# A gated recurrence on one Trainium2 core: the update gate's product with the state in seven half products, and one subtraction on GpSimd

## The chip, the core and the metric

The kernel runs on one core of one Trainium2 chip. Its engines are called as the profile calls them: PE (TensorE, the matrix engine), PEld (PE's weight loads), DVE (VectorE), ACT (ScalarE), POOL (GpSimd) and SP (the engine that issues most DMAs). The metric is the device time of one launch in microseconds (us), as the median of the runs.

## The reference, cut to what matters

The reference is one decoder layer in float32: causal self attention, then a slot attention with a gated recurrence (three rounds over the same 2048 rows of 256 features), then a mixture of experts. Only the recurrence matters here. Per round and per batch element:

```python
q_proj = rmsnorm(slots) @ Wq.T
scores = einsum('bkd,bmd->bkm', q_proj, k_proj) * SCALE
attn   = softmax(scores, axis=-2)                    # over the slots
attn   = attn / (sum(attn, axis=-1) + EPS)
updates = einsum('bkm,bmd->bkd', attn, v_proj)
# gru_cell(updates, slots):
gx = updates @ wih.T + bih          # split into xr, xz, xn
gh = slots @ whh.T + bhh            # split into hr, hz, hn
r = sigmoid(xr + hr)
z = sigmoid(xz + hz)
n = tanh(xn + r * hn)
slots = (1.0 - z) * n + z * slots
```

`slots` is 8 x 256 x 256 and the context `P` is 8 x 120 x 256, so an attention row has 120 entries.

## The kernel before, in words

**Stages.** Self attention fills the first 385 us of the profile, the recurrence the stretch from there to about 660 us, and the mixture of experts the rest.

**The recurrence in phases.** The rows lie feature-major in four blocks `XT[i]`, each 128 partitions x 2 chunks of features x 512 columns (two batch elements of 256). A phase `p` is one round for one block, so there are 12 phases, in the order round 0 block 0, 1, 2, 3, round 1 block 0, and so on. Phase `p` updates block `p % 4`, and a block is read again four phases later; its norm and scores are worked out two phases ahead (`norms(p + 2)`, `softmax(p + 2)`), its attention shares one phase ahead (`shares(p + 1)`).

The input side is folded: `G` (L773, filled by `given(b)`, L837) holds context x value weights x input weights, so that the product of the attention rows `AT_[p]` (120 x 512) with `G` gives the input part of a gate at once. In `gate(p, g, hidden, given)` (L903) a gate's sum of hidden and given part is built up in PSUM: per output chunk two matmuls of `whh_sb` with `XT[i]` over 512 columns, and two of `G` with `AT_[p]` over 256 columns each. In the profile each float32 matmul is two records.

**Seven products.** For the candidate's hidden part (g = 2) the 2 x 2 blocks of the weight (128 x 128 each) and of the state (128 x 256 each) are multiplied with seven block products instead of eight, in phases 0 to 8 (`SEVEN` = 9, `hidden_seven`, L964). The sums of weight blocks (`hidden_weights`, four POOL instructions into the finished `wih_sb`) are made once, the sums of state blocks (`hidden_states(p)`, four POOL instructions `t1` to `t4`) once a phase, in one of two sets `STATE_SUMS[p % 2]`. Four products go to a PSUM tile `x`, three to a second one `y`; ACT copies the first (L975), and four DVE instructions add the others into `out`, which is an SBUF tile. In phases 9 to 11 the plain `gate` is used.

**PSUM.** The gates and the seven products take tiles of two banks from the pool "big", which has two slots that are handed out in turn. A phase before phase 9 asks for five: the reset gate `r` (L992), `x` and `y` of the candidate, the candidate's given part `p_x` (L1006), and the update gate `p_z` (L1012). Smaller products (`pd`, `pr`, `pz`) use the pool "bk" of four banks.

**Order.** PE and ACT run in program order through the whole kernel (the manual schedule of L270). DVE and POOL do so only in the self attention (L275); in the recurrence the framework's planner orders their instructions when it builds the program, by its own estimate of when each becomes ready, and the engine then runs them in that order. In the profile POOL therefore works ahead: the squares for `norms(p + 3)` and the sums `hidden_states(p + 2)` are run in phase `p`.

**Within phase p**, in program order: `r` gate and its sigmoid (L994); `hidden_states(p + 1)` and `hidden_seven(p)`; the table of exponentials is loaded on ACT (L998); `shares(p + 1)`; L1002 turns `n` into (hn + bhh) * r on DVE; `norms(p + 2)` and `softmax(p + 2)`; `p_x`, added into `n` on DVE (L1007); the table of sigmoid and tanh (L1009); tanh (L1011); `p_z` and its sigmoid (L1014); then three DVE instructions, `r = sT - n`, `r = r * z` and `sT = r + n`, the last of which writes the block.

Of the kernel before, what the change touches and what calls it, by code (L numbers as in the profile page):

```python
# [14 lines left out]
ALU = mybir.AluOpType  # L15
AX = mybir.AxisListType

B, S, D = 8, 256, 256
# [4 lines left out]
P = 128  # L23
DC = D // P
# [3 lines left out]
BPB = BLK // S  # L28
# [37 lines left out]
def decoder_kernel(  # L66
# [23 lines left out]
    nc = tc.nc  # L90
# [6 lines left out]
    def big(name):  # L97
        return pools["big"].tile([P, 2, 512], F32, tag="big", name=name)

    def bank(name):  # L100
        return pools["bk"].tile([P, 512], F32, tag="bk", name=name)
# [38 lines left out]
    for c0 in (0, 256):  # L140
        nc.gpsimd.affine_select(
            out=mask[:, c0 : c0 + P],
# [33 lines left out]
    xwq_sb = const.tile([P, DC, D], F32, name="xwq_sb")  # L176
# [94 lines left out]
    with (  # L271
# [153 lines left out]
        def features(i, m, k):  # L425

            return XT[i][:, k, :].rearrange("p (t m q) -> p t m q", m=2, q=P)[:, :, m, :]
# [11 lines left out]
        def product(i, t, m):  # L439
            if V[i] is None:  # L440
                V[i] = a2.tile([P, NSUB, H * HD], F32, tag="v", name=f"v_{i}")
            pv = bank(f"pv_{i}_{t}_{m}")
            sums = [feature_sums[:, j, :] for j in range(4)]
            a11, a12, a22 = (features(i, *mk)[:, t, :] for mk in ((0, 0), (0, 1), (1, 1)))
            a, b = {
                1: (a11, B11),
                2: (a12, B21),
                3: (sums[3], B22),
                4: (a22, T4),
                5: (sums[0], T1),  # L450
                6: (sums[1], T2),
                7: (sums[2], T3),
            }[m]
            nc.tensor.matmul(pv, a, b, start=True, stop=True)
            c11, c12, c21, c22 = (V[i][:, 2 * t + n, c] for n in range(2) for c in half_cols)
            if m == 1:
                nc.scalar.copy(c11, pv)
            for o, old in {
                2: [(c11, c11)],
                3: [(c12, c12)],  # L460
                4: [(c21, c21)],
                5: [(c12, c22), (c22, c21)],
                6: [(c22, c11)],
                7: [(c21, c22)],
            }.get(m, []):
                nc.vector.tensor_tensor(o, pv, old, ALU.add)
# [176 lines left out]
        for k in range(last + 1):  # L643
            i, j = divmod(k, 2 * NPAIR)
# [50 lines left out]
    for table in (xd, yd):  # L695
# [21 lines left out]
        out=upper,  # L717
# [34 lines left out]
    for h in range(2):  # L752
        n = (NSINGLE + 1 - h) // 2
# [12 lines left out]
    def tt(o, a, b, op):  # L766
        nc.vector.tensor_tensor(o, a, b, op)  # L767
# [5 lines left out]
    G = b1.tile([MC, B, 3 * D], F32, name="G")  # L773
# [74 lines left out]
    RR, AT_ = {}, {}  # L848
# [54 lines left out]
    def gate(p, g, hidden, given):  # L903
        it, i = phases[p]
        pg = big(f"gate_{p}_{g}")
        for oc in range(DC):
            o = ts(DC * g + oc, P)
            if hidden:
                for dc in range(DC):
                    nc.tensor.matmul(  # L910
                        pg[:, oc, :],
                        whh_sb[:, dc, o],
                        XT[i][:, dc, :],
                        start=dc == 0,
                        stop=not given and dc == DC - 1,
                    )
            if given:
                for bi in range(BPB):
                    nc.tensor.matmul(  # L919
                        pg[:, oc, ts(bi, S)],  # L920
                        G[:, BPB * i + bi, o],
                        AT_[p][:, bi, :],
                        start=not hidden,
                        stop=not hidden or bi == BPB - 1,
                    )
        return pg
# [6 lines left out]
    SEVEN = len(phases) - NBLK + 1  # L933
    whh5 = whh_sb.rearrange("p k (g o q) -> p k g o q", o=DC, q=P)
    done = wih_sb.rearrange("p k n -> p (k n)")
    w_sums = done[:, 0 : 4 * P].rearrange("p (j q) -> p j q", q=P)
    STATE_SUMS = (
        [done[:, 4 * P + k * S :][:, 0:S] for k in range(4)],
        [w[:, k, :] for w in (xwk_sb, xwv_sb) for k in range(2)],
# [2 lines left out]
    def pool(o, a, b, op=ALU.subtract):  # L942
        nc.gpsimd.tensor_tensor(o, a, b, op)

    def hidden_weights():
        a11, a12, a21, a22 = (whh5[:, k, 2, o, :] for o in range(DC) for k in range(DC))
        s1, s2, s3, s4 = (w_sums[:, j] for j in range(4))
        pool(s1, a21, a22, ALU.add)
        pool(s2, s1, a11)
        pool(s3, a11, a21)  # L950
        pool(s4, a12, s2)

    def hidden_states(p):
        if p >= SEVEN:
            return
        it, i = phases[p]
        b11, b12, b21, b22 = (XT[i][:, k, ts(n, S)] for k in range(DC) for n in range(BPB))
        t1, t2, t3, t4 = STATE_SUMS[p % 2]
        pool(t1, b12, b11)
        pool(t2, b22, t1)  # L960
        pool(t3, b22, b12)
        pool(t4, b21, t2)

    def hidden_seven(p, out):  # L964
        it, i = phases[p]
        a11, a12, a21, a22 = (whh5[:, k, 2, o, :] for o in range(DC) for k in range(DC))
        s1, s2, s3, s4 = (w_sums[:, j] for j in range(4))
        b11, b12, b21, b22 = (XT[i][:, k, ts(n, S)] for k in range(DC) for n in range(BPB))
        t1, t2, t3, t4 = STATE_SUMS[p % 2]
        c = out.rearrange("p o (n s) -> p (o n) s", n=BPB)  # L970
        x, y = (big(f"seven_{p}_{j}").rearrange("p a (b q) -> p (a b) q", q=S) for j in range(2))
        for j, ab in enumerate(((a11, b11), (s3, t3), (a12, b21), (s2, t2))):
            nc.tensor.matmul(x[:, j], *ab, start=True, stop=True)

        nc.scalar.copy(c[:, 1], x[:, 0])  # L975
        tt(c[:, 0:2], x[:, 2:4], c[:, 1:2].to_broadcast([P, 2, S]), ALU.add)
        tt(c[:, 3], x[:, 1], c[:, 1], ALU.add)
        for j, ab in enumerate(((s4, b22), (a22, t4), (s1, t1))):
            nc.tensor.matmul(y[:, j], *ab, start=True, stop=True)
        tt(c[:, 1:3], y[:, 0:2], c[:, 1:4:2], ALU.add)  # L980
        tt(c[:, 1:4:2], y[:, 2:3].to_broadcast([P, 2, S]), c[:, 1:4:2], ALU.add)

    def phase(p, between):

        it, i = phases[p]
        sT = XT[i]

        def tmp(tag):
            return b2p.tile([P, DC, BLK], F32, tag=tag, name=f"{tag}_{p}")

        r, z, n = tmp("r"), tmp("z"), tmp("n")
        p_r = gate(p, 0, True, True)  # L992
        for oc in range(DC):
            nc.scalar.activation(r[:, oc, :], p_r[:, oc, :], AF.Sigmoid, bias=brz[:, oc : oc + 1])  # L994
        if p < SEVEN:
            hidden_states(p + 1)
            hidden_seven(p, n)
        nc.scalar.preload_act_table_set(LNEXP)  # L998
        between[0]()
        p_h = n if p < SEVEN else gate(p, 2, True, False)  # L1000
        for oc in range(DC):
            nc.vector.scalar_tensor_tensor(  # L1002
                n[:, oc, :], p_h[:, oc, :], bhh[:, 4 + oc : 5 + oc], r[:, oc, :], ALU.add, ALU.mult
            )
        between[1]()
        p_x = gate(p, 2, False, True)  # L1006
        tt(n, p_x, n, ALU.add)  # L1007
        between[2]()
        nc.scalar.preload_act_table_set(SIGTANH)  # L1009
        for oc in range(DC):  # L1010
            nc.scalar.activation(n[:, oc, :], n[:, oc, :], AF.Tanh, bias=bih[:, 4 + oc : 5 + oc])  # L1011
        p_z = gate(p, 1, True, True)  # L1012
        for oc in range(DC):
            nc.scalar.activation(z[:, oc, :], p_z[:, oc, :], AF.Sigmoid, bias=brz[:, 2 + oc : 3 + oc])  # L1014

        tt(r, sT, n, ALU.subtract)
        tt(r, r, z, ALU.mult)
        tt(sT, r, n, ALU.add)
        between[3]()
# [234 lines left out]
    for b in range(B):  # L1254
        given(b)
        if b in (1, 3):
            to_feature_major(NBLK - 2 + b // 2)
    shares(0)
    hidden_weights()
    hidden_states(0)  # L1260
    last = len(phases) - NBLK
# [143 lines left out]
    def tile_down(t):  # L1405
        row = TI.pop(t)[0]
        w1_sb, w2_sb, bt, b2t, e = TW.pop(t)
        n = groups(t)
        po = down(w2_sb, HT.pop(("t", t)), f"t{t}", groups=n)
        yo = f2.tile([P, 2, D], F32, tag="yo", name=f"yo_{t}")[:, 0:n, :]  # L1410
        tt(yo, po[:, 0:n, :], b2t.unsqueeze(1).to_broadcast([P, n, D]), ALU.add)
        return row, yo
# [82 lines left out]
    with tc.manual_schedule(engines={mybir.EngineType.SP}):  # L1495
        for k, t in enumerate(TILES):
# [5 lines left out]
            if k:  # L1502
                done = tile_down(TILES[k - 1])
# [46 lines left out]
    for a in range(half):  # L1550
        n = half + a
        down_group(po[a], shared[1], hT, a)
        z = Z[3][:, n : n + 1, :]
# [67 lines left out]
```

## Time and profile before

| what | value |
|---|---|
| median of 3 runs (lowest to highest) | 1086.99 us (1085.72 to 1089.74) |
| the profiled execution: time, span | 1053.3 us, 1051.5 us |
| mean granted PE clock | 0.999 |
| busy over the span: PE, DVE, ACT, POOL | 1034.5, 504.3, 425.2, 293.9 us |
| phase p = 6, 542.03 to 560.56 us: PE, DVE, ACT, POOL busy | 18.53, 11.13, 10.42, 7.08 us |
| phase p = 7, 560.56 to 579.10 us: PE, DVE, ACT, POOL busy | 18.54, 11.22, 10.42, 4.20 us |

The profiled execution took less than the timed runs, so durations are taken from the profile and set against its own span, and the difference is carried over to the median. The first phase's gate starts at 429.9 us, phase 9 at 597.6 us; in all views a time is counted from the start of the span. DVE and ACT records of neighbouring instructions may overlap by a tenth of a microsecond or less.

### The profile page before, as it was taken

What the parts mean: (1) busy time and instruction counts of PE and PEld (TensorE: products, weight loads), DVE (VectorE), ACT (ScalarE), POOL (GpSimd) and SP (SyncE); (2) the same over time, 40 slices, a digit from 0 to 9 for tenths busy, and PEclk for the clock granted to TensorE, in tenths of its full rate; (3) what the DMA queues carried; (4) which work ended last, traced back from release to release, by engine and by line L of the source; (5) the groups of instructions that cost most, each with busy time, mean ns of one, the idle gap of its engine ahead of it and who ended that gap; (6) DMA issues with size and microseconds to landing.
All of it is one profiled execution on the core that took longest, in us unless ns stands there. A gap on an engine that the chain in (4) does not pass through costs nothing. (4 is left out here: it accounts for less than half of the span.)

```text
span 1051.5 us, 14784 instructions
## 1 busy us (share of the span) xinstructions
PE 1034.5 (98%) x5156; PEld 771.3 (73%) x5156; DVE 504.3 (48%) x1552; ACT 425.2 (40%) x1183; POOL 293.9 (28%) x354
## 2 busy tenths in 40 slices
PE   9999999999999999999999999999999999999997
PEld 5556766766767775667666656888888888888886
DVE  4567676766677454356556558761010100101147
ACT  2345544544456403456556443532222223222232
POOL 4635433353333334234342103341000000000172
PEclk9999999999999999999999999999999999999999
DMA  9000000000001029996000001125667666754243
GB/s 303 12 2 1 1 1 2 1 1 2 1 1 36 26 91 380 348 349 218 1 0 1 1 1 37 44 82 200 229 217 244 213 211 219 247 195 134 69 122 102
DMA packets 91370, 114.17 MB, mean 109 GB/s; under 512 B 6751, under 2 KB 82335, under 8 KB 91295
## 3 DMA queue, kind: packets, MB, share of 16 engines
q1 hardware_dynamic: 87135, 102.72, 29.6%
q0 software_dynamic: 3072, 8.39, 2.4%
q10 hardware_dynamic: 1088, 2.10, 0.5%
q8 instruction: 42, 0.69, 0.3%
q14 instruction: 33, 0.27, 0.1%
HBM read 67.97 MB, written 45.22 MB: 108 GB/s over the span
## 5 line engine op out<-in xcount | busy, mean ns | idle before, releaser
L503 ACT ACTIVATE sc<-sc,nmax 128x128 f32<-128x128 f32 (+1 forms) x256 | 113.3, 444 | 147.3 <-DVE nmax L490 147.3
L518 POOL TENSOR_TENSOR sc<-sc,sums 128x256 f32<-128x256 f32 (+1 forms) x128 | 103.1, 827 | 180.1 <-DVE sums L515 136.5
L1301 ACT ACTIVATE hT_t<-ph_t,bt 128x256 f32<-128x256 f32 (+1 forms) x168 | 66.1, 444 | 193.0 <-issue 138.4
L1292 PE MATMUL ph_t<-xgT,w 128*128 128x256 f32 (+1 forms) x672 | 132.6, 356 | 0.8 <-ACT hT_t L1301 0.8
L1306 PE MATMUL pf_t<-w,hT_t 128*128 128x256 f32 x592 | 131.1, 380 | 0.0
L1292 PEld LDWEIGHTS ph_t<-xgT,w 128*128 128x128 f32 x672 | 116.4, 191 | 14.6 <-ACT hT_t L1301 1.0
L1306 PEld LDWEIGHTS pf_t<-w,hT_t 128*128 128x128 f32 x592 | 111.2, 190 | 14.1
L1425 POOL DMA_INDIRECT y<-yd,slot x32 | 30.7, 960 | 287.8 <-ACT hT_s L1301 278.4
L910 PE MATMUL gate<-XT,whh_sb 128*128 128x512 f32 x216 | 101.4, 593 | 0.0
L392 DVE TENSOR_TENSOR qk<-pq,qk 128x256 f32<-128x256 f32 x168 | 64.6, 420 | 39.5 <-ACT qk L390 29.1
L490 DVE CUSTOM_DVE_ANT_0 sc<-pp,mask 128x128 f32<-128x128 f32 (+1 forms) x256 | 75.2, 349 | 8.6 <-PE pp L478 7.6
L919 PEld LDWEIGHTS gate<-at,G 120*128 120x128 f32 x288 | 54.5, 190 | 29.8 <-issue 23.2
L1397 DVE COPY xgT<-xg 128x512 f32<-128x512 f32 (+1 forms) x21 | 13.2, 628 | 128.5 <-PE xg L1396 128.5
L919 PE MATMUL gate<-at,G 120*128 120x256 f32 x288 | 72.2, 379 | 0.4 <-DVE at L767 0.4
L767 DVE TENSOR_TENSOR yo<-pf_t,b2t 128x512 f32<-128x512 f32 (+1 forms) x21 | 13.2, 628 | 121.5 <-PE pf_t L1306 121.5
L910 PEld LDWEIGHTS gate<-XT,whh_sb 128*128 128x128 f32 x216 | 40.7, 190 | 31.1 <-issue 28.9
L548 PE MATMUL po<-pT,v 128*64 128x256 f32 (+1 forms) x512 | 55.8, 339 | 2.6 <-ACT pT L537 2.6
L1292 PE MATMUL ph_s<-XT,sh 128*128 128x256 f32 x256 | 57.6, 381 | 0.2
L564 PE MATMUL py<-wo_sb,ot 128*128 128x256 f32 x256 | 57.5, 380 | 0.0
L1306 PE MATMUL pf_s<-sh,hT_s 128*128 128x256 f32 x256 | 57.0, 380 | 0.0
L533 PE MATMUL pt<-ident,sc 128*128 128x128 f32 x384 | 56.0, 282 | 0.0
L548 PEld LDWEIGHTS po<-pT,v 128*64 128x64 f32 x512 | 31.1, 136 | 33.4 <-issue 17.6
(288 smaller groups left out, 1715.8 us busy)
## 6 DMA issues: line engine op xcount, KB each, us to landing
w<-in_ew_dram SPq DMA_DIRECT2D x42, 1024.0 KB, 5.5
xd<-zeros SPq DMA_DIRECT2D x1, 16640.0 KB, 54.6
yd<-zeros SPq DMA_DIRECT2D x1, 16640.0 KB, 103.8
xg<-xd SPq DMA_DIRECT2D x16, 256.0 KB, 5.0
yd<-yo SPq DMA_DIRECT2D x16, 256.0 KB, 5.6
b2t<-in_b_dram SPq DMA_DIRECT2D x21, 128.0 KB, 5.6
sh<-in_sh_w_dram SPq DMA_DIRECT2D x2, 1024.0 KB, 7.2
X<-in_x_dram SPq DMA_DIRECT2D x3, 512.0 KB, 11.6
```

The lines of the kernel that those rows point to most:

```text
L392: nc.vector.tensor_tensor(o, pq[:, ts(n, S)], old, ALU.add)
L490: nc.vector.tensor_tensor_reduce(out=sc[:, h, seg[t]], in0=pp[h][:, seg[t]], in1=mask[:, seg[t]], scale=-(HD**-0.5), scalar=3.0e38, op0=AL ...
L503: nc.scalar.activation(sc[:, h, seg[t]], sc[:, h, seg[t]], AF.Exp, scale=-1.0, bias=nmax[:, t, h : h + 1], accum_out=sums[:, t, h : h + 1],)
L518: nc.gpsimd.tensor_tensor(sc[:, :, seg[t]], sc[:, :, seg[t]], sums[:, t, :].unsqueeze(2).to_broadcast([P, 2, w]), ALU.mult,)
L533: nc.tensor.transpose(pt[:, ts(c, P)], sc[:, h, ts(c, P)], ident)
L548: nc.tensor.matmul(po[ts(h, HD), q0:S], V[i][:, 2 * bi + c, ts(2 * pr + h, HD)], pT[:, h, 0:S] if c == 0 else pT[:, h, S:384], start=c == ...
L564: nc.tensor.matmul(py, OT[i][:, pr, ts(n, P)], wo_sb[:, pr, :], start=pr == 0, stop=pr == NPAIR - 1)
L910: nc.tensor.matmul(pg[:, oc, :], whh_sb[:, dc, o], XT[i][:, dc, :], start=dc == 0, stop=not given and dc == DC - 1,)
L919: nc.tensor.matmul(pg[:, oc, ts(bi, S)], G[:, BPB * i + bi, o], AT_[p][:, bi, :], start=not hidden, stop=not hidden or bi == BPB - 1,)
L1292: nc.tensor.matmul(ph[:, a, 0:width], w1_sb[:, dc, ts(c, P)], rhs(dc), start=dc == 0, stop=dc == DC - 1,)
L1301: nc.scalar.activation(hT[:, c, 0:width], ph[:, a, 0:width], AF.Gelu_apprx_tanh, bias=bias[:, c : c + 1])
L1306: nc.tensor.matmul(po, hT[:, c, ts(a, P)], w2_sb[:, c, :], start=c == 0, stop=c == FC - 1)
```

## The change

In phases 0 to 8 the hidden part of the update gate is also formed with seven block products, by the same function, which now takes the gate's number `g`. The four sums of weight blocks for g = 1 are made beside those for g = 2 and kept in `xwq_sb`, whose last reader is `attention_joined` (L799) ahead of the phases. The state sums are shared by the two gates.

For g = 1 the given part is added on PE into the same PSUM tiles: into product `x[2]`, into `y[0]` and `y[1]`, and into a fourth part `y[3]` of its own. ACT copies two products at once (128 x 512) instead of one, POOL adds one pair of 256 columns in SBUF in place of DVE, and DVE has one more addition at the end. The result is in the SBUF tile `z`, and the sigmoid then works in place. A phase before phase 9 asks for six tiles of "big" instead of five.

In these phases `r = sT - n` moves from DVE to POOL.

```diff
-    w_sums = done[:, 0 : 4 * P].rearrange("p (j q) -> p j q", q=P)
+    w_sums = {
+        2: done[:, 0 : 4 * P].rearrange("p (j q) -> p j q", q=P),
+        1: xwq_sb.rearrange("p k (j q) -> p (k j) q", q=P),
+    }
...
     def hidden_weights():
-        a11, a12, a21, a22 = (whh5[:, k, 2, o, :] for o in range(DC) for k in range(DC))
...
+        for g in (2, 1):
+            a11, a12, a21, a22 = (whh5[:, k, g, o, :] for o in range(DC) for k in range(DC))
+            s1, s2, s3, s4 = (w_sums[g][:, j] for j in range(4))
+            pool(s1, a21, a22, ALU.add)
+            pool(s2, s1, a11)
+            pool(s3, a11, a21)
+            pool(s4, a12, s2)
...
-    def hidden_seven(p, out):
+    def hidden_seven(p, g, out):
...
+        given = g == 1
+
+        def product(dst, ab, *block):
+            more = given and bool(block)
+            if ab:
+                nc.tensor.matmul(dst, *ab, start=True, stop=not more)
+            if more:
+                o, n = block
+                weights = G[:, BPB * i + n, ts(DC * g + o, P)]
+                nc.tensor.matmul(dst, weights, AT_[p][:, n, :], start=not ab, stop=True)
+
+        product(x[:, 0], (a11, b11))
+        product(x[:, 1], (s3, t3))
+        product(x[:, 2], (a12, b21), 0, 0)
+        product(x[:, 3], (s2, t2))
+
+        if given:
+            nc.scalar.copy(c[:, 1:4:2], x[:, 0:2])
+        else:
+            nc.scalar.copy(c[:, 1], x[:, 0])
         tt(c[:, 0:2], x[:, 2:4], c[:, 1:2].to_broadcast([P, 2, S]), ALU.add)
-        tt(c[:, 3], x[:, 1], c[:, 1], ALU.add)
...
+        if given:
+            pool(c[:, 3], c[:, 3], c[:, 1], ALU.add)
+        else:
+            tt(c[:, 3], x[:, 1], c[:, 1], ALU.add)
+        product(y[:, 0], (s4, b22), 0, 1)
+        product(y[:, 1], (a22, t4), 1, 0)
+        product(y[:, 2], (s1, t1))
+        product(y[:, 3], None, 1, 1)
         tt(c[:, 1:3], y[:, 0:2], c[:, 1:4:2], ALU.add)
         tt(c[:, 1:4:2], y[:, 2:3].to_broadcast([P, 2, S]), c[:, 1:4:2], ALU.add)
+        if given:
+            tt(c[:, 3], y[:, 3], c[:, 3], ALU.add)
...
-        p_z = gate(p, 1, True, True)
+        if p < SEVEN:
+            hidden_seven(p, 1, z)
+        p_z = z if p < SEVEN else gate(p, 1, True, True)
         for oc in range(DC):
             nc.scalar.activation(z[:, oc, :], p_z[:, oc, :], AF.Sigmoid, bias=brz[:, 2 + oc : 3 + oc])
 
-        tt(r, sT, n, ALU.subtract)
+        (pool if p < SEVEN else tt)(r, sT, n, ALU.subtract)
         tt(r, r, z, ALU.mult)
         tt(sT, r, n, ALU.add)
```

More of the change, by code (lines that the diff above doesn't have):

```diff
@@ L945, in hidden_weights @@
     def hidden_weights():
-        a11, a12, a21, a22 = (whh5[:, k, 2, o, :] for o in range(DC) for k in range(DC))
[L947 to L951, printed above, removed]
+        for g in (2, 1):
[5 more added lines that the diff above has]
+            pool(s4, a12, s2)
     def hidden_states(p):
@@ L962, in hidden_states @@
         pool(t4, b21, t2)
-    def hidden_seven(p, out):
+    def hidden_seven(p, g, out):
         it, i = phases[p]
-        a11, a12, a21, a22 = (whh5[:, k, 2, o, :] for o in range(DC) for k in range(DC))
-        s1, s2, s3, s4 = (w_sums[:, j] for j in range(4))
+        a11, a12, a21, a22 = (whh5[:, k, g, o, :] for o in range(DC) for k in range(DC))
+        s1, s2, s3, s4 = (w_sums[g][:, j] for j in range(4))
         b11, b12, b21, b22 = (XT[i][:, k, ts(n, S)] for k in range(DC) for n in range(BPB))
@@ L970, in hidden_seven @@
         c = out.rearrange("p o (n s) -> p (o n) s", n=BPB)
[L971 to L975, printed above, removed]
-        tt(c[:, 0:2], x[:, 2:4], c[:, 1:2].to_broadcast([P, 2, S]), ALU.add)
-        tt(c[:, 3], x[:, 1], c[:, 1], ALU.add)
-        for j, ab in enumerate(((s4, b22), (a22, t4), (s1, t1))):
-            nc.tensor.matmul(y[:, j], *ab, start=True, stop=True)
+        x, y = (big(f"seven_{p}_{g}_{j}").rearrange("p a (b q) -> p (a b) q", q=S) for j in range(2))
+        given = g == 1
[15 more added lines that the diff above has]
+            nc.scalar.copy(c[:, 1], x[:, 0])
+        tt(c[:, 0:2], x[:, 2:4], c[:, 1:2].to_broadcast([P, 2, S]), ALU.add)
+        if given:
[6 more added lines that the diff above has]
+        product(y[:, 3], None, 1, 1)
         tt(c[:, 1:3], y[:, 0:2], c[:, 1:4:2], ALU.add)
         tt(c[:, 1:4:2], y[:, 2:3].to_broadcast([P, 2, S]), c[:, 1:4:2], ALU.add)
+        if given:
+            tt(c[:, 3], y[:, 3], c[:, 3], ALU.add)
     def phase(p, between):
@@ L996, in phase @@
             hidden_states(p + 1)
-            hidden_seven(p, n)
+            hidden_seven(p, 2, n)
         nc.scalar.preload_act_table_set(LNEXP)
```

## The prediction

> **What bounds the kernel now.** First the page's busy times and a table of stretches: is PE waiting anywhere in the recurrence? Columns of the stretches: from:to, length, then busy time (records) of PE, PEld, DVE, ACT, POOL, the granted PE clock, DMA.
>
> ```profile
> PE 1034.5 (98%) x5156; PEld 771.3 (73%) x5156; DVE 504.3 (48%) x1552; ACT 425.2 (40%) x1183; POOL 293.9 (28%) x354
> ...
> 384.00:404.00 20.00, 18.93 (x70) 11.32 (x69) 14.59 (x23) 2.68 (x6) 15.29 (x33) 1.00 0.90 306
> 542.03:560.56 18.53, 18.53 (x68) 12.43 (x66) 11.13 (x15) 10.42 (x17) 7.08 (x7) 1.00 0.00 1
> 560.56:579.10 18.54, 18.54 (x68) 12.45 (x67) 11.22 (x15) 10.42 (x17) 4.20 (x3) 1.00 0.00 0
> ```
>
> A phase is 18.53 us and PE is busy for all of it: PE alone sets the phase, so matmul time taken out counts only if nothing else becomes the slowest loop. So I read the timeline of phase 7 next, PE's weight loads, then ACT, then DVE (start, us, engine, line; R = 560.56 is the phase's start).
>
> ```profile
> 573.92 0.41 PEld L910 LDWEIGHTS gate<-XT,whh_sb 128*128 128x128 f32 x2
> 574.57 0.19 PEld L910 LDWEIGHTS gate<-XT,whh_sb 128*128 128x128 f32 x1 [0.24 <-issue]
> 579.09 0.41 PEld L910 LDWEIGHTS gate<-XT,whh_sb 128*128 128x128 f32 x2
> ...
> 567.87 0.37 ACT L975 COPY n<-seven 128x256 f32<-128x256 f32 x1 [0.46 <-PE seven L973]
> 575.52 1.28 ACT L1009 ACT_TABLE_LOAD   x1
> 576.82 1.34 ACT L1011 ACTIVATE n<-n,vec_sb 128x512 f32<-128x512 f32 x2
> 579.51 1.26 ACT L1014 ACTIVATE z<-gate,brz 128x512 f32<-128x512 f32 x2 [1.36 <-PE gate L919]
> ...
> 568.27 2.67 DVE L767 TENSOR_TENSOR n<-seven,n 128x512 f32<-128x512 f32 x4 [3.44 <-ACT n L975]
> 570.98 0.75 DVE L1002 SCALAR_TENSOR_TENSOR n<-n,vec_sb,r 128x512 f32<-128x512 f32 x1
> 574.34 1.23 DVE L767 TENSOR_TENSOR n<-gate,n 128x1024 f32<-128x1024 f32 x1
> ```
>
> The update gate occupies PE from 573.92 to the next phase's first load at 579.09. Tanh is not over until 578.16. It hangs on a chain that starts with the candidate's products: ACT copy 567.87, DVE without a pause from 568.27 to the maxima at 574.32, exponentials, table load 575.52, tanh. The chain has been harmless because the next phase's `r` gate takes the slot of `p_x`, empty since 575.57.
>
> **The change part by part. PE.** Loads of 128x512 matmul records follow each other at 0.43 us (574.57 to 575.00), those of 256 columns at 0.215, so a half product costs exactly half. The update gate was 4 matmuls of 512 (8 records, 3.44) and 4 of 256 (8 records, 1.72): 5.16. Now it is 7 + 4 matmuls of 256, 22 records: 4.73. Saved: 0.43 a phase, 3.9 over nine phases. That is all the gain there is; `y[3]` is a given part that was there before.
>
> **The new slot order.** Six tiles a phase instead of five: `r` A, candidate `x` B, `y` A, `p_x` B, update `x` A, `y` B, and the next `r` takes A, the slot of the update gate's `x`. It is free only when ACT's copy and DVE's first addition have read it, and the copy stands behind tanh in ACT's program order. In phase 7:
> - ACT copy of 128x512 from PSUM: 0.585 (L111, same shape), directly behind tanh, with the 0.09 by which the two tanh records (2 x 0.714 in 1.34) overlap: 578.07 to 578.65. Bounds: 0.37 (the 256 copy) to 0.6.
> - DVE's first addition 0.69 (the candidate's twin), 0.03 after the copy as at 568.27: 578.68 to 579.37. DVE is free there, since `r = sT - n` has left.
> - PE's restart 0.05 later (phase 0: DVE ends 432.60, PE starts 432.65): 579.42.
>
> PE would have been ready at 573.92 + 4.73 = 578.65. It waits 0.77 and the next phase starts at 579.42, not 579.09: +0.33 a phase. Everything on PE is queued behind that wait, and the chain above restarts from it, so it repeats nine times: +3.0. The saving is inside this number.
>
> `y` of the update gate needs slot B from `p_x`: free 575.57, wanted 573.92 + 5 x 0.43 = 576.07. No wait; in phases 0 to 6 this margin is about 0.25 instead.
>
> **POOL and the rest of z.** `r = sT - n` on POOL: 2.36, by the nearest row of 128x1024 with two inputs, against 1.23 on DVE:
>
> ```profile
> L559 POOL TENSOR_TENSOR X<-X,bo_sb 128x1024 f32<-128x1024 f32 x4 | 9.4, 2361 | 15.6 <-PE pv L399 10.7 <-PE xt L221 4.9
> L943 POOL TENSOR_TENSOR wih_sb<-XT,wih_sb 128x256 f32<-128x256 f32 x10 | 7.3, 730 | 0.6
> L1002 DVE SCALAR_TENSOR_TENSOR n<-n,vec_sb,r x18: 736/748/1125, 441.2 to 590.8; 128x512 f32<-128x512 f32 x18
> ```
>
> It becomes ready first and runs 578.22 to 580.58; the new 256-column addition follows, 0.73, to 581.33. DVE waits for it, then adds `y` three times (0.69, 0.69, 0.42) to 583.27. Sigmoid of z (1.26, starts after the second) to 584.13, `r * z` to 585.39, `sT` to 586.71. Measured from the new phase start that is +7.29; before, the block was ready at 582.13 + 1.22, +4.26. Who needs it? The candidate's four additions on DVE begin at +7.71, so they are not held up, by 0.42. ACT's sigmoid of the next `r` stands behind z's sigmoid; it is due at +5.58 and z's ends at +4.71. Slot B (`y`) is free at +3.85 and wanted at +5.17. These covers are thin: 0.4 to 1.3 us.
>
> **Contention, which pays and costs.** L1002's first record takes 1.12 in phases 0 to 6 and 0.75 in phases 7 and 8. In the former POOL is running `t` sums beside it, in the latter there are none. With the change these sums wait for the update gate's products, which read them too, and move to about +1.9 to +4.9 of the next phase, clear of L1002: 0.37 of the chain comes back in phases 0 to 6, so the calculation on phase 7 holds for all. But POOL's squares move as well: 0.08 after the block, 1.89 + 0.08 + 1.27, they end at +10.61, and L1002 starts at +10.42. In phase 6 an overlap of 0.57 (552.45 to 553.02) cost 0.37; 0.19 costs about 0.12. Eight times: +1.0. The Trainium skill (SBUF — State Buffer, section Who interferes with whom) says that a DVE instruction with two SBUF inputs is blocked fully by a GpSimd instruction that reads SBUF. By that the phase-6 record would have lost the whole 0.57; it lost 0.37. I take the row. By the rule this term is 8 x 0.19 = 1.5. The additions on PSUM data are untouched: the candidate's four last 2.67 with sums beside them (549.74) and without (568.27).
>
> **The clock.** The Trainium skill (TensorE: Matmul & The Clock Gate, section A second HAM failure mode: psum-queue depth-cycling) speaks against this change: PE pausing briefly between groups while it cycles through PSUM buffers can make its clock swing between half and full speed, over windows of about 3.4 us. One such window per phase at half speed would lose 1.7 us, 15 in all. The row against it: from 384 to 404 us PE is idle for 1.07 us in pieces and the granted clock is 1.00. Pauses of 0.77 are like these; I take the row, at nothing.
>
> **Costed at nothing.** Four more weight sums on POOL, 4 x 0.45 = 1.8, at 395 us: POOL is idle from 400.7 to 407.6 and they are first read at 444; without that cover they would delay the first softmax by up to 1.8 once. DVE's extra additions (+2.5, -1.23) fall into its idle time, which is over 7 us a phase. No DMA moves.
>
> **The sum.** Against the profiled execution (span 1051.5, time 1053.3): -3.9 saved on PE, +6.9 waits for slot A (9 x 0.77), +1.0 for the squares: +4.0, less perhaps 0.9, as the first matmul after a pause in phase 0 followed 0.1 sooner on its load. I take +3.6. The median of the timed runs is 33.7 above the profiled time, and nothing ties that to the recurrence; carried over, 1086.99 + 3.6 = 1090.6.
>
> **The rivals.** (a) The wait is no wait: the copy's data is read early, PE never stops, and the full 3.9 comes: 1083.1. For it, PE's 98%; against it, tanh ends at 578.16 and the copy is behind it. A gain can't pass 3.9.
> (b) The sums or something else on POOL stay beside L1002, and phases 0 to 6 keep 1.12: another 7 x 0.25, with the squares overlapping all of L1002 in phases 1 to 8 up to 8 x 0.37 = 3.0 instead of 1.0: 1092 to 1093.5.
> (c) Slower, by POOL's order, which the planner fixes: one released sum (`t1`, free when the update gate's third `y` product is done, about 578.6) is put ahead of `r = sT - n`. Then that starts 1.05 later and all behind it: the block is ready at +8.34, past +7.71, the candidate's additions wait 0.63 and the squares then overlap L1002 by 0.58 (0.37). A phase costs 0.33 + 0.63 + 0.37 = 1.33: 8 x 1.33 + 0.33 = 11, 1098. It decides as soon as the z path is 0.42 later than worked out. For it, that slim margin; against it, `r = sT - n` is ready 0.4 us earlier and comes earlier in the program.
>
> **How the numbers follow.** About 0.5% (5.4 us) is what a measurement of this kernel can tell from no change. The forecast, +2 to +5.4: 0.47. (a) or a partial wait, below +2: 0.12, of it 0.03 below -5.4 by drift between runs. (b), +5 to +8: 0.2, most of it above 5.4. (c) and longer: 0.21. So faster 0.03, same 0.55, slower 0.42. The range leaves out half of (a) and the far half of (c): 1086 to 1099.
>
> **What would show it.** In a changed profile: the update gate's 22 records at 0.215; a PE gap of 0.7 to 0.9 ahead of each `r` gate of phases 1 to 9, released by DVE's addition; a phase of about 18.9; L1002 near 0.75 to 0.9 throughout; POOL's subtraction at 2.36 right behind tanh. Phases below 18.4 with no gap, or above 19.5, prove me wrong; the latter with the candidate's additions waiting for `sT` is (c).

## The result and the profile after

The changed kernel took 1096.14 us (median of 7 runs, 1091.55 to 1099.86) against 1085.72 us for the kernel before (7 runs beside it). The ratio is 1.009, with a 95% interval of 1.007 to 1.0109: about 10 us slower, where +3.6 had been forecast. Its profiled execution has a span of 1093.3 us at a mean granted clock of 0.986, against 1051.5 us and 0.999 for the one profile of before. Only 11.5 us of that difference lie in the recurrence; 30.6 us lie behind it (from phase 9's `pd` to the end 479.4 us against 448.7). The kernel before itself took 1053.6 us on one chip, beside `e1`, `e2`, `e4` and `e5` below, and 1081.35 us on another, beside `e3`, `e6`, `e7` and `e8`, so times are compared only by the ratio to the kernel before run beside them, and profiles by the recurrence alone.

First the busy times of the whole kernel and the table of stretches, in the columns that the prediction explains, for phases 4 and 5 of the changed kernel:

```profile
PE 1046.3 (96%) x5210; PEld 782.0 (72%) x5210; DVE 516.3 (47%) x1579; ACT 430.7 (39%) x1192; POOL 322.7 (30%) x376
...
509.15:529.38 20.23, 19.13 (x72) 13.25 (x72) 12.46 (x17) 10.86 (x18) 10.07 (x10) 1.00 0.00 1
529.38:549.61 20.23, 19.13 (x72) 13.24 (x73) 12.45 (x17) 10.87 (x18) 10.06 (x10) 1.00 0.00 0
```

A phase that lasted 18.53 us with PE never idle now lasts 20.23 with PE idle for 1.10. That idle time is less than PE's waiting, since the record of one matmul runs past the start of the next. Counted from one weight load to the next, PE waits 1.36 us ahead of each `r` gate in the middle phases (1.57 between two loads that otherwise follow at 0.215) and 0.3 to 0.45 at three more places. The granted clock stays at 1.00. Which waits are these? Some of the waits of the stretch from 430 to 660 us (engine, line, waited for; total us, times, longest):

```profile
ACT z L1044 <- DVE z L767: 42.4, 8, 5.7
DVE z L767 <- POOL z L946: 27.1, 9, 3.4
PEld gate L910 <- DVE z L767: 11.2, 9, 1.4
PEld seven L982 <- DVE n L767: 2.9, 7, 0.5
PEld seven L982 <- ACT r L1022: 2.8, 6, 0.5
```

The third line is the forecast wait, nine times, ahead of each `r` gate. The first two are the path of `z`: DVE waits up to 3.4 us for POOL's addition, and ACT's sigmoid waits for DVE. The last two were not forecast. Rows of the timeline around the end of phase 3 show the order on POOL (phase 4 starts with the load at 509.15):

```profile
505.30 0.30 PEld L982 LDWEIGHTS seven<-XT,xwq_sb 128*128 128x128 f32 x2 [0.46 <-DVE n L767]
506.57 1.34 ACT L1039 ACTIVATE n<-n,vec_sb 128x512 f32<-128x512 f32 x2
507.81 0.56 ACT L994 COPY z<-seven 128x512 f32<-128x512 f32 x1
507.98 2.35 POOL L946 TENSOR_TENSOR r<-XT,n 128x1024 f32<-128x1024 f32 x1 [1.41 <-ACT n L1039]
508.41 0.69 DVE L767 TENSOR_TENSOR z<-seven,z 128x512 f32<-128x512 f32 x1 [2.95 <-ACT z L994]
509.15 0.30 PEld L910 LDWEIGHTS gate<-XT,whh_sb 128*128 128x128 f32 x2 [1.39 <-DVE z L767]
510.29 0.73 POOL L946 TENSOR_TENSOR xwk_sb<-XT 128x256 f32<-128x256 f32 x1
511.09 0.72 POOL L946 TENSOR_TENSOR xwk_sb<-XT,xwk_sb 128x256 f32<-128x256 f32 x1
511.77 0.72 POOL L946 TENSOR_TENSOR z<-z 128x256 f32<-128x256 f32 x1
512.53 1.88 DVE L767 TENSOR_TENSOR z<-seven,z 128x512 f32<-128x512 f32 x3 [3.43 <-POOL z L946]
514.04 1.34 ACT L1044 ACTIVATE z<-z,brz 128x512 f32<-128x512 f32 x2 [5.67 <-DVE z L767]
514.52 0.30 PEld L982 LDWEIGHTS seven<-XT,whh_sb 128*128 128x128 f32 x2 [0.34 <-issue]
515.41 1.22 DVE L767 TENSOR_TENSOR r<-r,z 128x1024 f32<-128x1024 f32 x1 [1.00 <-ACT z L1044]
516.55 0.37 ACT L996 COPY n<-seven 128x256 f32<-128x256 f32 x1
516.59 0.30 PEld L982 LDWEIGHTS seven<-XT,wih_sb 128*128 128x128 f32 x2 [0.47 <-ACT r L1022]
516.67 1.22 DVE L767 TENSOR_TENSOR XT<-r,n 128x1024 f32<-128x1024 f32 x1
517.81 2.66 DVE L767 TENSOR_TENSOR n<-seven,n 128x512 f32<-128x512 f32 x4
517.97 1.89 POOL L856 TENSOR_TENSOR sq<-XT 128x1024 f32<-128x1024 f32 x1 [4.79 <-DVE XT L767]
519.95 1.27 POOL L857 TENSOR_TENSOR sq<-sq 128x512 f32<-128x512 f32 x1
520.51 1.26 DVE L1030 SCALAR_TENSOR_TENSOR n<-n,vec_sb,r 128x512 f32<-128x512 f32 x1
```

Up to 509.15 this is the forecast's picture: tanh, copy, DVE's first addition, PE's restart 0.05 later. Behind the subtraction, however, POOL does not run the addition `z<-z`, which has been ready since 509.10. It runs two of the sums for the phase after next (`xwk_sb`, `t1` and `t2` of phase 5), and the addition starts only at 511.77. All of `z` moves with it. The block is written at 516.67 to 517.89, so the candidate's four additions on DVE start at 517.81, although ACT's copy for them was done at 516.92. The squares on POOL, behind the block, then lie over L1030, which takes 1.26 instead of 0.75. L1030 is on the chain to tanh, tanh on the chain to the next phase.

### The profile page after: what moved, and what is told of

It reads as the page before. It is cut to its first block, busy times and chain, and to the rows that moved or that the text cites. A ratio compares the mean times of both kernels' runs of the same rounds, so it can differ in the third digit from the quotient of the medians.

```text
span 1093.3 us, 14932 instructions
## 1 busy us (share of the span) xinstructions
PE 1046.3 (96%) x5210; PEld 782.0 (72%) x5210; DVE 516.3 (47%) x1579; ACT 430.7 (39%) x1192; POOL 322.7 (30%) x376
## 5 line engine op out<-in xcount | busy, mean ns | idle before, releaser
L1322 PE MATMUL ph_s<-XT,sh 128*128 128x256 f32 x256 | 63.1, 397 | 13.9 <-issue 11.8
L910 PE MATMUL gate<-XT,whh_sb 128*128 128x512 f32 x144 | 68.4, 600 | 7.6 <-DVE z L767 7.6
L1336 PE MATMUL pf_s<-sh,hT_s 128*128 128x256 f32 x256 | 59.6, 390 | 8.6 <-issue 8.6
L1322 PEld LDWEIGHTS ph_s<-XT,sh 128*128 128x128 f32 x256 | 49.9, 198 | 24.9 <-issue 15.8
L1331 ACT ACTIVATE hT_s<-ph_s,vec_sb 128x256 f32<-128x256 f32 x64 | 26.9, 472 | 91.3 <-PE ph_s L1322 52.2
L1336 PEld LDWEIGHTS pf_s<-sh,hT_s 128*128 128x128 f32 x256 | 49.9, 197 | 16.0 <-issue 9.0
L919 PEld LDWEIGHTS gate<-at,G 120*128 120x128 f32 x216 | 40.9, 189 | 20.3 <-issue 14.6
```

Source lines behind the costliest of these rows:

```text
L910: nc.tensor.matmul(pg[:, oc, :], whh_sb[:, dc, o], XT[i][:, dc, :], start=dc == 0, stop=not given and dc == DC - 1,)
L919: nc.tensor.matmul(pg[:, oc, ts(bi, S)], G[:, BPB * i + bi, o], AT_[p][:, bi, :], start=not hidden, stop=not hidden or bi == BPB - 1,)
L1322: nc.tensor.matmul(ph[:, a, 0:width], w1_sb[:, dc, ts(c, P)], rhs(dc), start=dc == 0, stop=dc == DC - 1,)
L1331: nc.scalar.activation(hT[:, c, 0:width], ph[:, a, 0:width], AF.Gelu_apprx_tanh, bias=bias[:, c : c + 1])
L1336: nc.tensor.matmul(po, hT[:, c, ts(a, P)], w2_sb[:, c, :], start=c == 0, stop=c == FC - 1)
```

## The experiments

Each was timed beside the kernel before. "Phase" is the distance between the weight loads of L898 (`pd`) in successive phases, once a phase in each kernel; the middle phases are given. It is 18.53 us before and 20.23 after; over phases 0 to 9 these distances sum to 163.8 and 175.3 us, so the recurrence became 11.5 us longer. For every kernel but `e8` the interval of the ratio takes in what this sum gives; for `e8` the sum gives -3.6 us and the interval -4.5 to -7.4.

| kernel | addition | subtraction | copy and tanh | phase, us | ratio to before | 95% interval |
|---|---|---|---|---|---|---|
| after | POOL, behind two sums | POOL | tanh first | 20.23 | 1.009 | 1.007 to 1.0109 |
| `e1_add_on_dve` | DVE | POOL | tanh first | 18.67 | 1.0009 | 1.0002 to 1.0016 |
| `e7_add_first` | POOL, ahead of the sums | POOL | tanh first | 18.73 | 1.002 | 1.0007 to 1.0033 |
| `e2_diff_on_dve` | POOL, behind three sums | DVE | tanh first | 19.76 | 1.0093 | 1.0077 to 1.0108 |
| `e3_both_on_dve` | DVE | DVE | tanh first | 19.39 | 1.0077 | 1.0063 to 1.009 |
| `e4_only_diff` | (no seven products for z) | POOL | | 18.53 | 0.9998 | 0.9989 to 1.0006 |
| `e5_copy_before_tanh` | POOL, ahead of the sums | POOL | copy first | 18.13 | 0.996 | 0.9947 to 0.9974 |
| `e6_copy_early_add_dve` | DVE | POOL | copy first | 18.13 | 0.9956 | 0.9943 to 0.997 |
| `e8_copy_early_diff_dve` | POOL, ahead of the sums | DVE | copy first | 18.13 | 0.9945 | 0.9932 to 0.9958 |

**The addition on DVE.**

```diff
         if given:
-            pool(c[:, 3], c[:, 3], c[:, 1], ALU.add)
+            tt(c[:, 3], c[:, 3], c[:, 1], ALU.add)
```

> The 256-column addition of the update gate goes back from POOL to DVE; all else as in the changed kernel. Theory 1 (the addition stands on POOL behind the 2.35 us subtraction and two state sums, so z, the block and the candidate's additions come late): without that queue the phases 1 to 6 fall from 20.23 to the 18.87 us that the wait for slot A alone gives, R(0) to R(9) about 170.5 us, the kernel +3 us against before (the new addition may still be held until the subtraction on POOL ends, about 1.2 us, which the z path has room for). Rival (the subtraction on POOL itself, by its port and its length, is what delays the phase): it is still there, so phases stay near 20.2 and the kernel stays at +10.

Measured: 18.67 us a phase, ratio 1.0009, about +1 us. Theory 1 holds, though the phase is 0.2 shorter than the 18.87 expected (why, see the wait for slot A in the next section). The rival falls: the subtraction is still on POOL, at its full length. Rows of this kernel's timeline:

```profile
504.25 2.35 POOL L946 TENSOR_TENSOR r<-XT,n 128x1024 f32<-128x1024 f32 x1 [1.20 <-ACT n L1039]
504.68 0.69 DVE L767 TENSOR_TENSOR z<-seven,z 128x512 f32<-128x512 f32 x1 [2.95 <-ACT z L994]
505.40 1.48 DVE L767 TENSOR_TENSOR z<-z 128x256 f32<-128x256 f32 x1
505.42 0.30 PEld L910 LDWEIGHTS gate<-XT,whh_sb 128*128 128x128 f32 x2 [0.68 <-DVE z L767]
511.48 1.22 DVE L767 TENSOR_TENSOR XT<-r,n 128x1024 f32<-128x1024 f32 x1
513.02 2.67 DVE L767 TENSOR_TENSOR n<-seven,n 128x512 f32<-128x512 f32 x4 [0.32 <-ACT n L996]
515.73 0.84 DVE L1030 SCALAR_TENSOR_TENSOR n<-n,vec_sb,r 128x512 f32<-128x512 f32 x1
```

The addition, two inputs in SBUF, is held by the subtraction until about 506.5, as expected (1.48 for an operation that takes 0.42 in `e3_both_on_dve`), and there is still room: the block is done 0.32 before the candidate's additions want DVE, and L1030 takes 0.84. What remains is PE's wait of 0.68 for slot A.

**Place or engine?** In `e1_add_on_dve` the addition leaves the queue and the engine at once. This kernel keeps it on POOL and moves only the sums behind it (`issue_after` sets the order on the queue):

```diff
-            pool(c[:, 3], c[:, 3], c[:, 1], ALU.add)
+            ADDED[p] = nc.gpsimd.tensor_tensor(c[:, 3], c[:, 3], c[:, 1], ALU.add)
...
-        pool(t1, b12, b11)
-        pool(t2, b22, t1)
+        def sums():
+            pool(t1, b12, b11)
+            pool(t2, b22, t1)
+            pool(t4, b21, t2)
+
         pool(t3, b22, b12)
-        pool(t4, b21, t2)
+        if p - 2 in ADDED:
+            with tc.issue_after(ADDED[p - 2].ins):
+                sums()
+        else:
+            sums()
```

> The changed kernel with one thing different: the three state sums t1, t2, t4 are queued on POOL behind the update gate's 256-column addition instead of two of them ahead of it; the addition and the subtraction stay on POOL. Theory 1 (the place in the queue is the cause): phases 1 to 6 fall from 20.23 to about 18.75 us (18.67 as with the addition on DVE, and a little for the squares beside L1030), +2 us in all against before. Rival (the engine is the cause: POOL is slower and its traffic blocks DVE wherever the addition stands): phases stay above 19.5, +8 us or more.

Measured: 18.73 us, ratio 1.002, about +2 us. In its timeline the addition starts right behind the subtraction:

```profile
504.57 2.35 POOL L946 TENSOR_TENSOR r<-XT,n 128x1024 f32<-128x1024 f32 x1 [1.26 <-ACT n L1048]
506.88 0.73 POOL L1008 TENSOR_TENSOR z<-z 128x256 f32<-128x256 f32 x1
507.56 0.73 POOL L946 TENSOR_TENSOR xwk_sb<-XT 128x256 f32<-128x256 f32 x1
511.77 1.22 DVE L767 TENSOR_TENSOR XT<-r,n 128x1024 f32<-128x1024 f32 x1
513.34 2.67 DVE L767 TENSOR_TENSOR n<-seven,n 128x512 f32<-128x512 f32 x4 [0.34 <-ACT n L1005]
```

Two sums ahead of one addition cost 1.5 us a phase; the engine itself costs 0.06 (18.73 against 18.67). The place in the queue is thus shown to be the cause of the miss.

**The subtraction.** Back on DVE with the addition on POOL, and both on DVE:

```diff
-        (pool if p < SEVEN else tt)(r, sT, n, ALU.subtract)
+        tt(r, sT, n, ALU.subtract)
```

> The subtraction sT - n goes back from POOL to DVE; the 256-column addition stays on POOL, now planned behind the state sums. Theory 1: DVE runs the subtraction (1.23) before the update gate's first addition, so slot A comes free 0.8 later than with it on POOL: phases of about 19.65 us also in phases 7 and 8, +10 us in all. Rival (the subtraction on POOL is what costs): phases of 18.9 or less, +3 us or better.

> Both the subtraction and the 256-column addition on DVE, so the change is the seven products alone. Theory 1: as with the subtraction alone on DVE (19.76 us a phase), since DVE runs it ahead of the update gate's first addition and slot A waits for that: about +11 us. Rival (the addition on POOL is the only cost of the change): 18.7 us a phase, +1 to +3.

Measured: 19.76 and 19.39 us, ratios 1.0093 and 1.0077. The first is near the 19.65 expected; the second beat the 19.76 and +11 expected of it by 0.37 a phase. The rival of each falls. With the copy late and the addition on DVE, the subtraction on POOL even pays: 18.67 in `e1_add_on_dve` against 19.39 in `e3_both_on_dve`. Rows of `e2_diff_on_dve`, then of `e3_both_on_dve`:

```profile
527.21 1.23 DVE L767 TENSOR_TENSOR r<-XT,n 128x1024 f32<-128x1024 f32 x1 [2.48 <-ACT n L1039]
528.35 0.68 DVE L767 TENSOR_TENSOR z<-seven,z 128x512 f32<-128x512 f32 x1
530.59 0.73 POOL L946 TENSOR_TENSOR z<-z 128x256 f32<-128x256 f32 x1
538.76 1.27 POOL L857 TENSOR_TENSOR sq<-sq 128x512 f32<-128x512 f32 x1
539.40 1.18 DVE L1030 SCALAR_TENSOR_TENSOR n<-n,vec_sb,r 128x512 f32<-128x512 f32 x1
...
535.97 1.27 POOL L857 TENSOR_TENSOR sq<-sq 128x512 f32<-128x512 f32 x1
538.42 0.75 DVE L1030 SCALAR_TENSOR_TENSOR n<-n,vec_sb,r 128x512 f32<-128x512 f32 x1
```

In both kernels DVE runs the subtraction (1.23) ahead of the update gate's first addition, and PE waits for that. The 0.37 between them lies in L1030: in `e2_diff_on_dve` the addition stands on POOL behind all three sums, the block is late and the squares lie beside L1030, which takes 1.18; in `e3_both_on_dve` the squares are done before it, and it takes 0.75.

Moved alone, in the kernel before, the subtraction changes nothing, as expected (18.53 us, ratio 0.9998):

> The kernel before with only the subtraction sT - n moved to POOL in phases 0 to 8. Theory 1: PE still sets the phase at 18.53 us, the subtraction (2.35 instead of 1.23) ends before z's sigmoid does, no change: 0 within 1.5 us. Rival (the subtraction on POOL costs by itself): 5 us or more.

**The wait for slot A.** The update gate's products are written ahead of tanh; PE's order stays as it is, and ACT's copy stands between the table load and tanh:

```diff
         nc.scalar.preload_act_table_set(SIGTANH)
+        if p < SEVEN:
+            hidden_seven(p, 1, z)
         for oc in range(DC):
             nc.scalar.activation(n[:, oc, :], n[:, oc, :], AF.Tanh, bias=bih[:, 4 + oc : 5 + oc])
-        if p < SEVEN:
-            hidden_seven(p, 1, z)
```

> The changed kernel with the update gate's products written ahead of tanh, so that ACT copies x after its table load and before tanh; both POOL operations stay. Theory 1: slot A is free at 17.6 us of a phase, before PE wants it at 18.1; no PE wait, phases of 18.10, R(0) to R(9) 163.8 us, -3.9 us against before. Rival (PE's short waits are not the cause, or the port contention on POOL holds the phase): phases above 18.5, no gain over before.

Measured: 18.13 us a phase, ratio 0.996 (0.9947 to 0.9974), 4 us faster than before. Rows of the timeline:

```profile
499.81 1.28 ACT L1037 ACT_TABLE_LOAD   x1
501.10 0.59 ACT L994 COPY z<-seven 128x512 f32<-128x512 f32 x1
501.58 1.33 ACT L1041 ACTIVATE n<-n,vec_sb 128x512 f32<-128x512 f32 x2
501.72 0.69 DVE L767 TENSOR_TENSOR z<-seven,z 128x512 f32<-128x512 f32 x1 [1.73 <-ACT z L994]
502.49 0.73 POOL L946 TENSOR_TENSOR z<-z 128x256 f32<-128x256 f32 x1 [1.18 <-DVE z L767]
502.60 0.41 PEld L986 LDWEIGHTS seven<-at,G 120*128 120x128 f32 x2
503.03 0.41 PEld L910 LDWEIGHTS gate<-XT,whh_sb 128*128 128x128 f32 x2
503.17 2.36 POOL L946 TENSOR_TENSOR r<-XT,n 128x1024 f32<-128x1024 f32 x1
```

Slot A is read out at 502.41; PE wants it at 503.03 and does not stop (the load follows the one before it at the usual 0.43). Tanh is 0.5 us later, and the phase shows no cost of it. This edit also put the addition ahead of subtraction and sums on POOL, since it was ready before them. Two more kernels keep the early copy and put one or the other operation back on DVE:

> ACT's copy ahead of tanh, and the 256-column addition on DVE. Theory 1: PE sets the phase again at 18.13 us whatever engine adds: -3.6 to -4.2 us against before, as with the addition on POOL. Rival (the gain with the early copy came from the addition's better place in POOL's queue): here it should be no better than with the addition on DVE and a late copy, +1.

> ACT's copy ahead of tanh, and the subtraction on DVE (it then stands behind the update gate's first addition there). Theory 1: slot A is free before PE wants it, so the subtraction on DVE costs nothing: 18.13 us a phase, -3.6 to -4.2 us. Rival (GpSimd's help with the subtraction is needed for any gain): 18.5 us or more.

Measured: 18.13 us in both, ratios 0.9956 and 0.9945 (-4.8 and -5.9 us). The phase is the 18.13 of theory 1 in both, and both rivals fall; the time of the second kernel fell by more than the phases explain. With the copy early it does not matter which engine subtracts or adds; PE sets the phase again. All three beat both the kernel before and the changed one; their intervals overlap, so none of them is shown to be the best.

## Why the prediction was wrong, point by point

- **PE's saving**: right. 0.43 a phase was worked out; with nothing in the way (`e5_copy_before_tanh`) the phase falls from 18.53 to 18.13, by 0.40.
- **The new slot order and the wait for slot A**: right in mechanism, nine times, released by DVE's first addition. Alone (`e1_add_on_dve`) it made the phase 0.14 longer than before, not 0.33: PE waited 0.68 instead of 0.77, and after the pause the `r` gate's loads took 5.06 us to the candidate's first instead of 5.17. That is the 0.1 a phase which the sum named as "perhaps". In the changed kernel itself this wait is 1.36, since the late addition delays tanh and with it the copy.
- **POOL and the rest of z**: the step that failed. "The new 256-column addition follows" the subtraction: it did not. The planner had put two sums between, and the addition started 1.4 us later than that step put it (511.77, where the subtraction ended at 510.33). The cover of 0.42 in front of the candidate's additions was gone, as the prediction said it would be with `z` that late. Against `e1_add_on_dve`, where they start 7.60 after the phase's start, they start 8.66 after it; L1030 takes 1.26 instead of 0.84. Together that is 1.48 of the 1.56 by which 20.23 exceeds 18.67.
- **Contention**: the relief was right (0.75 to 0.89 for this instruction in `e1_add_on_dve`, `e3_both_on_dve` and `e7_add_first`, where the addition is in time), and so was the direction of the cost. The squares were taken at 0.19 of overlap and 0.12 of delay; they lay over L1030 for 0.71 (520.51 to 521.22) and cost about 0.5.
- **Covers**: ACT's sigmoid of `z` was to end at +4.71 with 0.9 to spare. It ended at +6.2, and the `r` sigmoid behind it held PE for 0.47; slot B was late for the candidate's `x` (0.34; the profile names no releaser here, but DVE's last addition of `y` ends just before, at 514.41), and `p_x` left slot B late for the update gate's `y` (0.46). None was forecast, and all follow from the late addition: in `e1_add_on_dve` and `e7_add_first` PE goes through these places at its usual distance.
- **The clock**: taken at nothing, rightly: it is 1.00 in phases with PE idle for 1.10 us. The 15 us that the prediction set against it are an estimate from windows of about 3.4 us; the Trainium skill gives these on the page that the prediction names (TensorE: Matmul & The Clock Gate), but in its section What's actually happening.
- **The rivals**: (c) had the mechanism, POOL's order makes `z` late by more than the cover, and nearly its price: 1.33 a phase above the kernel before, where 1.70 was measured. It had the wrong instructions waiting: one sum ahead of the subtraction, where it was two sums between the subtraction and the addition. It was given 0.21, since it was argued only from what is ready first. That the stated range reaches the measured time at all is owed to (c). The terms of (b), 7 x 0.25 and 2.0 more on top of 1090.6, add up to 1092.3 to 1094.3, not to its 1093.5. That the planner runs sums and squares a phase early was in the profile of before; that a short addition, which becomes ready in the middle of a long subtraction (at 509.10), shares the queue with sums whose buffers come free before that (the third `y` product ends at 507.74), should have been weighed as the likeliest case.
- **The sum**: +3.6 was forecast. `e7_add_first`, the kernel that the forecast described, gives about +2. The other 8 to 10 us are the queue.

## What to carry to other kernels

Before an operation is moved to a quieter engine, write down that engine's queue for the moment when it becomes ready: what runs ahead because it was free to, and who stands behind the result. Where a planner sets that order, read it before counting on it, or pin the order of the few instructions on the critical loop. And when a change adds a buffer to a rotation of two, ask first who empties the slot that the next stage now gets: here, one copy moved ahead of tanh on ACT took the phase from 18.67, the best with the copy behind tanh, to 18.13, and after that the choice of engine for the addition and the subtraction no longer mattered.

## What the runs showed of the hardware that had not been expected

In the profile of the changed kernel PE stands still behind the recurrence, in the mixture of experts, in stretches like these (us, then PE busy and, before the last two columns, the granted clock):

```profile
720.00:740.00 20.00, 12.75 (x48) 10.85 (x49) 1.40 (x5) 3.16 (x8) 6.50 (x7) 0.74 0.57 193
1040.00:1060.00 20.00, 12.16 (x34) 8.28 (x34) 6.21 (x17) 3.11 (x8) 11.26 (x12) 0.59 0.25 73
```

PE is idle for 7 to 8 us in each of these stretches without a releaser that the profile shows, and the clock is lower there. In the first PE stops at 718.7 for 8.6 us in one piece, while the granted clock is 1.00 until 721.7 and 0.50 from there to 731.9; in the second no piece is longer than 2.2 us. Pauses of about 1 us once in each phase of 20 us left it at 1.00. In the profile of the kernel before PE never stops there for more than 1.5 us. What makes these gaps stays open.

A DVE instruction with two inputs in SBUF lost less time than it shared with a POOL instruction's record: L1030 at 520.51 took 0.51 more than its 0.75, though the squares' record ran on for 0.71, and the addition of `e1_add_on_dve` took 1.06 more than its 0.42 beside 1.20 of the subtraction's. Whether the hold ends early or POOL's records end late, no run here shows.
